# A convolutional-attention layer's preparation: all box differences on VectorE, and the first area addition behind the unit length of v

## The chip, the cores and the metric

The kernel runs on one core of one Trainium2 chip. A core has five engines with an instruction queue each: TensorE (PE in the profile; its weight loads are PEld), VectorE (DVE), ScalarE (ACT), GpSimd (POOL) and SyncE (SP, which here only starts transfers). An engine works through its queue in order and waits on semaphores for the others. The metric is the device time of one execution in microseconds (us). The time before is the median of three runs.

## The reference, cut to what matters

The input is an image of 256 channels and 64 x 64 places. A group normalisation goes ahead of layer 0, a box attention with 8 heads of 32 channels; layer 1 is a softmax attention over the 4096 places followed by a routed feed-forward layer with 8 experts. The change touches layer 0 alone:

```python
q = sigmoid(x . Wq);  k = sigmoid(x . Wk);  v = x . Wv / max(norm(v per head), 1e-12)
Ik  = integral(k)                   # sums over rows and columns
Ikv = integral(k[d] * v[f])         # the same for each product of channels
for w in (1, 2, 4):                 # box of 64/w x 64/w places, edges held
    wk, wkv = box(Ik), box(Ikv)     # four corners of the integral
    attn = sum_d q[d] * wkv[d, f]
    norm = sum_d q[d] * wk[d]
    outs.append(attn / (norm + 1e-6))
x = x + concat(outs) . Wout + bout
```

A box sum is taken by differences of prefix sums: along one axis, the prefix sum at the far end less the one at the near end; past the image's edge the last prefix sum (the "whole") stands for the far end.

## The kernel before

Layer 0 is done twice, for group 0 and group 1 of 128 channels (4 heads each): `prepare(g)` makes queries, keys, values and denominators, `attend(g)` the masked products within the boxes. The image is cut into NCH = 8 strips of SW = 8 columns; a strip is NB = 4 tiles of 16 x 8 = 128 places, each of two cells of 8 x 8. The three boxes reach REACH = 4, 2 and 1 strips to each side.

`prepare` consists of these steps, in the order of the program:

1. Keys and values (L441 on PE), eight times: the sigmoid of keys on ACT (L453), the copy of values on DVE (L454), their squares on POOL (L455), sums of squares on DVE (L456). After each half, a root on ACT (L459), then on DVE a maximum (L460), a reciprocal (L461) and the scaling of `v` to length 1 (L463, the whole half at once).
2. Sums of `k v` by cell (`sum_cells`, L418 on PE), in four parts. The last two parts need the second half of `v` scaled; they stand in PE's queue behind the area products 1 and 2. ACT copies them to `st` (L430).
3. Area products, one for each strip `ix` (L536 and L540 on PE): prefix sums of keys within the strip. DVE adds what lies left of the strip (`side`): L544 for the 64 rows, L547 for the row below, L549 for the next `side`. In group 0, strips 1 to 4 are followed by 8 transposes each (`residual`, L385), which are held behind that strip's L549 by `tc.issue_after(latest.ins)`. They read rows to which ACT has added a bias (L379).
4. Cell sums become prefix sums (`near`, L490 and L493 on DVE), then half boxes for reach 4 and 2: a copy on ACT (L503) and two differences (L506, L512) along each axis. In group 0 the two differences run on POOL, in group 1 on DVE:

```python
engine = nc.vector if g else nc.gpsimd
```

5. Query and key projections by channel (L476 on PE, a sigmoid on ACT, L483), four pairs of strips each.
6. For each reach, `tall` and `edge`: differences of the area along rows (an ACT copy L581, DVE L584 and L586). Then, for two blocks of four strips, `prod`: the difference along columns, times q. Where the near end lies left of the image there is no difference (L598, DVE). Elsewhere the difference is on POOL (L602 from the whole, L604 between two strips) and the product on DVE (L605). PE adds the products of all channels of a head into the denominators (L609), and DVE reads them when all three boxes are in (L622).

`prod` has two buffers, and shares them with `st` and the half boxes. `tall` has one. The PSUM tiles of steps 1, 2, 3 and 5 come from one ring of three (two banks each), so an area product needs the additions of an earlier one done.

Instructions are put on the engines' queues by a scheduler that goes by what is ready in its own estimate, so the order on DVE isn't the order of the program: in group 0, additions of strips 0 and 1 were put ahead of the second scaling of `v`. `tc.issue_after(x)` keeps what is recorded under it behind `x`. Transfers are not moved: SP's queue is the same before and after.

`attend` begins when the denominators are read (L622). Its masks are multiplied on DVE and POOL (L659), both before and after.

Of the kernel before, what the change touches and what calls it, by code (L numbers as in the profile page):

```python
# [30 lines left out]
P = 128  # L31
# [3 lines left out]
NT = N // P  # L35
CH = 512
NCH = N // CH
IMG = 64
SW = 8
# [3 lines left out]
D = 32  # L43
# [77 lines left out]
def tile_conv_attn_hybrid(ctx: ExitStack, tc: tile.TileContext, a: dict, out: bass.AP):  # L121
    nc = tc.nc
# [99 lines left out]
    def tok(i):  # L222
        return slice(P * i, P * (i + 1))
# [44 lines left out]
    with ExitStack() as phase:  # L268
# [124 lines left out]
        def prepare(g, w3, prep, ps):  # L393
# [41 lines left out]
            ss = prep.tile([P, 4 * NT], F32, name="ss")  # L435
            for i4 in range(0, NT, 4):
                pr = two_banks()
                kv = pr.rearrange("p j (i n o) -> p (j i) n o", i=2, n=2)
                for i in range(4):
                    for k in range(KC):  # L440
                        nc.tensor.matmul(  # L441
                            kv[:, i],
                            act[:, k, tok(i4 + i)],
                            w3[:, k, 1:3, :],
                            start=k == 0,
                            stop=k == KC - 1,
                        )
                at = slice(i4, i4 + 4)

                with ExitStack() as order:  # L450
                    if not g and i4 >= NT - 8:
                        order.enter_context(tc.issue_after(biased((i4 - NT + 8) // 4)))
                    nc.scalar.activation(kt[:, at, :], kv[:, :, 0, :], AF.Sigmoid)  # L453
                nc.vector.tensor_copy(v[:, at, :], kv[:, :, 1, :])  # L454
                nc.gpsimd.tensor_mul(sq[:, at, :], v[:, at, :], v[:, at, :])  # L455
                nc.vector.tensor_reduce(ss[:, 4 * i4 : 4 * (i4 + 4)], heads(sq[:, at, :]), AX.X, ALU.add)  # L456
                if i4 % 16 == 12:
                    half = slice(4 * (i4 - 12), 4 * (i4 + 4))
                    rooted = nc.scalar.sqrt(ss[:, half], ss[:, half])  # L459
                    nc.vector.tensor_scalar_max(ss[:, half], ss[:, half], 1e-12)  # L460
                    nc.vector.reciprocal(ss[:, half], ss[:, half])  # L461
                    to = heads(v[:, i4 - 12 : i4 + 4, :])
                    latest = nc.vector.tensor_mul(to, to, ss[:, half].unsqueeze(2).to_broadcast([P, 2 * NT, D]))  # L463
                if i4 >= NT - 8:
                    sum_cells((i4 - NT + 8) // 4)

# [19 lines left out]
            def near():  # L486


                for i in range(1, NCH):
                    nc.vector.tensor_add(st[:, i], st[:, i], st[:, i - 1])  # L490
                    yield
                for i in range(1, SW):
                    nc.vector.tensor_add(st[:, :, i], st[:, :, i], st[:, :, i - 1])  # L493
                    yield

                engine = nc.vector if g else nc.gpsimd

                def boxes(to, src, r, axis):

                    along = (lambda z, s: z[:, s]) if axis == 0 else (lambda z, s: z[:, :, s])  # L500
                    cut = lambda n: [P, n, SW, D] if axis == 0 else [P, SW, n, D]
                    last = lambda n: along(src, slice(SW - 1, SW)).to_broadcast(cut(n))
                    nc.scalar.copy(along(to, slice(0, r)), along(src, slice(r - 1, 2 * r - 1)))  # L503
                    n = SW + 1 - 2 * r
                    if n > 0:
                        engine.tensor_sub(  # L506
                            along(to, slice(r, r + n)),
                            along(src, slice(2 * r - 1, SW)),
                            along(src, slice(0, n)),
                        )  # L510
                    n = max(n, 0)
                    engine.tensor_sub(  # L512
                        along(to, slice(r + n, SW)), last(SW - r - n), along(src, slice(n, SW - r))
                    )

                for r in REACH[:2]:
                    half = prep.tile([P, NCH, SW, D], F32, tag="st", name="half", bufs=2)
                    boxes(half, st, r, 0)
                    yield
                    boxes(ssum[r], half, r, 1)  # L520
                    yield
# [6 lines left out]
            area = prep.tile([P, NCH, IMG + 1, SW], F32, tag="area", name="area")  # L528
            new_side = lambda: prep.tile([P, IMG + 1], F32, tag="side", name="side", bufs=2)
            side = new_side()  # L530
            nc.vector.memset(side, 0.0)
            for ix in range(NCH):
                pr = two_banks()
                for m in range(NB):
                    lhsT = kt[:, NB * ix + m, :]
                    nc.tensor.matmul(  # L536
                        pr[:, 0, P * m :], lhsT, ck["before8"][:, : CH - P * m], start=m == 0, stop=m == NB - 1
                    )
                    n = SW + IMG + 1
                    nc.tensor.matmul(  # L540
                        pr[:, 1, :n], lhsT, ck["sides"][:, n * m : n * (m + 1)], start=m == 0, stop=m == NB - 1
                    )
                left = side.unsqueeze(2).to_broadcast([P, IMG + 1, SW])
                nc.vector.tensor_add(  # L544
                    area[:, ix, :IMG, :], pr[:, 0, :].rearrange("p (y c) -> p y c", c=SW), left[:, :IMG]
                )
                nc.vector.tensor_add(area[:, ix, IMG, :], pr[:, 1, :SW], left[:, IMG])  # L547
                upto = new_side()
                add = nc.vector.tensor_add(upto, pr[:, 1, SW:n], side)  # L549
                side, latest = upto, add if ix else latest  # L550
                if ix in (1, 2):
                    sum_cells(ix + 1)
                if not g and 1 <= ix <= NB:
                    with tc.issue_after(latest.ins):
                        residual(ix - 1)
                for _ in range(3 if ix > 1 else 0):
                    next(steps, None)
# [11 lines left out]
            for w, r in enumerate(REACH):  # L569
# [18 lines left out]
                y_c = lambda z: z.rearrange("p (y c) -> p y c", c=SW)  # L588
                whole = edge.unsqueeze(2).to_broadcast([P, IMG, SW])
                for lo in range(0, NCH, 4):  # L590
                    prod = prep.tile([P, 4, CH], F32, tag="st", name="prod", bufs=2)
                    at = lo
                    while at < lo + 4:
                        first, last = at < r, at + r >= NCH
                        n = 1 if at + 1 in (r, NCH - r, lo + 4) else 2
                        to, of = prod[:, at - lo : at - lo + n], lambda by: sums[:, at + by : at + by + n]
                        if first:
                            nc.vector.tensor_mul(to, of(r), q[:, at : at + n])  # L598
                        else:
                            if last:  # L600
                                for j in range(n):
                                    nc.gpsimd.tensor_sub(y_c(to[:, j]), whole, y_c(of(-r)[:, j]))  # L602
                            else:
                                nc.gpsimd.tensor_sub(to, of(r), of(-r))  # L604
                            nc.vector.tensor_mul(to, to, q[:, at : at + n])  # L605
                        at += n
                    for i in range(lo, lo + 4):
                        n = NCH // 4 * w + i // 4
                        nc.tensor.matmul(  # L609
                            den[D * (i % 4) : D * (i % 4 + 1), :],  # L610
                            ck["sums"][:, D * n : D * (n + 1)],
                            prod[:, i - lo, :],
                            start=w == 0 and lo == 0,
                            stop=w == NW - 1 and lo > 0,
                            skip_group_check=True,
                        )
                    if later:
                        later.pop(0)()
# [18 lines left out]
        turns, latest, owed = [0], [None], [0]  # L637
# [234 lines left out]
        for g in range(KC):  # L872
            with tc.tile_pool(name="c_prep", bufs=1) as prep, psum("c_ps1", 2) as ps:
                of = prepare(g, w3, prep, ps)
# [284 lines left out]
    with ExitStack() as phase:  # L1159
# [590 lines left out]
        with tc.If(tame > 0) as branch:  # L1750
            with (
# [108 lines left out]
                held, latest, turned = [], [], []  # L1860
# [41 lines left out]
                r, i, room = slots.pop(0)  # L1902
                for cost, ops in pieces:
                    if cost is None:
                        while not (r % KC == KC - 1 and i in (13, 25)) or (r, i) in early:
                            r, i, room = slots.pop(0)
                        shared[r, i] = ops
                        r, i, room = slots.pop(0)
                        continue
                    if cost > room:  # L1910
                        r, i, room = slots.pop(0)
# [15 lines left out]
                for s, (r, i) in enumerate(places):  # L1927
                    qc, g = rounds[r]
# [34 lines left out]
                for n in range(CH // P):  # L1963
                    to = result(KC - 1, NCH - 1)[:, tok(n)]
# [5 lines left out]
        with branch.Else():  # L1970


            with (
# [8 lines left out]
                for hd in range(2 * 4):  # L1982
                    g, hs = hd // 4, slice(D * (hd % 4), D * (hd % 4 + 1))
# [116 lines left out]
```

## Time and profile before

| | |
|---|---|
| median of 3 runs | 2748.64 us (2747.01 to 2750.99) |
| the profiled execution | 2748.26 us, span 2746.5 us |
| mean granted TensorE clock | 0.984 |
| busy: PE, DVE, ACT, POOL | 96%, 68%, 55%, 32% of the span |
| POOL busy | 887.4 us in 953 instructions |
| preparation of group 0, from the first projection to the denominators (L441 to L622) | 22.3 to 143.4 us |
| preparation of group 1, the same | 517.5 to 623.5 us |
| layer 1 and what follows | from about 1042 us to the end |

A profile line names the line of the kernel, the engine, the operation and its tiles (out, then in) with partitions x elements. A mean of a group mixes shapes, so durations are best taken shape by shape. Starts and durations in the timeline are in us; what stands in brackets is the engine's idle time just before and what released it. Back to back, instructions of DVE overlap by some 0.1 us, so the sum of durations is a little more than the time they take. [...]

### The profile page before, as it was taken

The page shows a single profiled execution, that of the slowest core. Times are in us where ns is not written, and L with a number is a line of the kernel's source. Part 1 is how long each engine was busy: PE and PEld are TensorE (multiplying, and loading weights), DVE is VectorE, ACT ScalarE, POOL GpSimd, SP SyncE. Part 2 cuts the span into 40 slices and gives each one's busy share as a digit, 9 for nine tenths or more (in the row PEclk, how much of TensorE's full clock was granted, in tenths as well). Part 3 has the DMA queues.
Part 4 walks back from the last instruction along what each step waited for, and adds up shares of the span by engine and source line. Part 5 has one row for each costly group of instructions (what it writes and reads, how often), then busy time and mean ns, then how long its engine had stood idle before and what let it go on. Part 6 is the DMA issues. An engine that isn't in the chain of part 4 may idle for free.

```text
span 2746.5 us, 71816 instructions
## 1 busy us (share of the span) xinstructions
PE 2638.5 (96%) x30910; PEld 1187.3 (43%) x30910; DVE 1878.5 (68%) x2520; ACT 1503.2 (55%) x2083; POOL 887.4 (32%) x953
## 2 busy tenths in 40 slices
PE   6889999988999999999999999999999999999995
PEld 5454336745433655111212121212121278888884
DVE  5758788675868876788888889888888871111114
ACT  3223323222232334999898989898989852222222
POOL 2558777435777742000000100000001123222220
PEclk9899999999999999999999999999999999999996
DMA  5000000000000000455555555555656645555555
GB/s 146 7 23 21 15 26 24 8 13 23 24 12 28 22 21 1 99 118 117 112 113 113 116 113 113 113 113 116 132 113 132 159 142 180 190 187 178 187 175 194
DMA packets 114468, 256.66 MB, mean 93 GB/s; under 512 B 19890, under 2 KB 76440, under 8 KB 100052
## 3 DMA queue, kind: packets, MB, share of 16 engines
q0 software_dynamic: 22240, 132.66, 23.1%
q1 hardware_dynamic: 84724, 110.30, 12.4%
q10 hardware_dynamic: 7168, 8.92, 1.0%
q8 instruction: 247, 4.05, 0.6%
q14 instruction: 89, 0.73, 0.1%
HBM read 118.64 MB, written 17.86 MB: 50 GB/s over the span
## 4 chain that ended last, share of the span: by engine, by line
PE 90%; DVE 4%; DMA 3%; issue 1%; POOL 1%; ACT 0%; ACTq 0%; SPq 0%; DVEq 0%; POOLq 0%
PE ps_three L1805 19%; PE ps_acc L1764 18%; PE ps_sc L832 8%; PE ps_yp L1473 7%; PE ps_hp L1456 7%; PE ps_acc L848 7%; PE ps_sc L732 3%; PE ps_sc L759 3%; PE ps_acc L790 3%; PE ps_two L441 2%; PE ps_mm L1248 2%; DMA yrows<-v,qk 2%; PE ps_two L536 1%; PE ps_acc L778 1%; PE ps_two L476 1%
## 5 line engine op out<-in xcount | busy, mean ns | idle before, releaser
L1805 PE MATMUL ps_three<-qk 32*64 32x512 f32 x6144 | 564.0, 613 | 2.0 <-DVE t L1743 1.0
L1805 PE MATMUL ps_one<-qk 32*64 32x512 f32 x2048 | 557.2, 613 | 0.2 <-ACT pe L1814 0.2
L652 ACT COPY sm<-ps_sc 128x384 f32<-128x384 f32 (+3 forms) x454 | 218.5, 511 | 525.5 <-PE ps_sc L832 333.9
L1837 DVE TENSOR_TENSOR act<-act,pe 128x2048 f32<-128x2048 f32 x195 | 446.9, 2292 | 83.6 <-ACT pe L1817 53.1
L1817 ACT ACTIVATE pe<-ps_three 128x1536 f32<-128x1536 f32 x330 | 477.4, 1447 | 0.0
L1825 POOL DMA_DIRECT2D pe<-pe x108 | 93.3, 863 | 940.4 <-ACT pe L1817 654.6
L659 DVE TENSOR_TENSOR sm<-ps_sc,mask 128x512 f32<-128x512 f32 (+3 forms) x740 | 340.4, 520 | 68.4 <-PE ps_sc L832 65.2
L659 POOL TENSOR_TENSOR sm<-sm,mask 128x192 f32<-128x192 f32 (+3 forms) x428 | 350.1, 848 | 113.3 <-ACT sm L652 112.9
L1837 DVE TENSOR_TENSOR act<-act 128x2048 f32<-128x2048 f32 x150 | 343.9, 2292 | 51.1 <-ACT act L1817 37.9
L1764 PE MATMUL ps_acc<-pe,v 128*32 128x512 f32 x2640 | 352.4, 606 | 0.0
L1459 ACT ACTIVATE v<-ps_hp,qk 128x256 f32<-128x256 f32 (+1 forms) x256 | 123.0, 480 | 343.5 <-PE ps_hp L1456 340.7
L1805 PEld LDWEIGHTS ps_three<-qk 32*64 32x64 f32 x6144 | 112.8, 130 | 415.0 <-ACT pe L1814 242.3
L1817 ACT ACTIVATE act<-ps_three 128x1536 f32<-128x1536 f32 x182 | 263.1, 1446 | 0.0
L1473 PE MATMUL ps_yp<-qk,v 128*128 128x256 f32 (+1 forms) x1088 | 241.7, 380 | 0.0
L1456 PE MATMUL ps_hp<-qk 128*128 128x256 f32 (+1 forms) x1024 | 237.6, 389 | 2.8 <-ACT v L1459 1.7
L832 PE MATMUL ps_sc<-qk 32*64 32x384 f32 (+3 forms) x3584 | 235.2, 458 | 0.5 <-issue 0.5
L1814 ACT ACTIVATE pe<-ps_one 128x512 f32<-128x512 f32 x330 | 197.4, 598 | 60.9 <-PE ps_one L1805 36.8
L1473 PEld LDWEIGHTS ps_yp<-qk,v 128*128 128x128 f32 (+1 forms) x1088 | 200.3, 187 | 30.7 <-issue 1.3
L848 PE MATMUL ps_acc<-sm,v 128*32 128x256 f32 (+3 forms) x2688 | 213.2, 419 | 0.2
L1456 PEld LDWEIGHTS ps_hp<-qk 128*128 128x128 f32 x1024 | 181.0, 189 | 53.3 <-ACT v L1459 14.2
L1764 PE MATMUL ps_acc<-act,v 128*32 128x512 f32 x1456 | 193.9, 604 | 0.0
L659 DVE TENSOR_TENSOR sm<-ps_sc,ycut 128x384 f32<-128x384 f32 (+4 forms) x254 | 129.1, 560 | 81.5 <-PE ps_sc L759 79.8
(365 smaller groups left out, 2946.3 us busy)
## 6 DMA issues: line engine op xcount, KB each, us to landing
pe<-pe POOLq DMA_DIRECT2D x108, 1024.0 KB
qk<-in_L_ffn_W SPq DMA_DIRECT2D x64, 1024.0 KB
by<-recs SPq DMA_DIRECT2D x48, 256.0 KB
rows<-in_x SPq DMA_DIRECT2D x16, 256.0 KB
qk<-in_L_ffn_b SPq DMA_DIRECT2D x32, 128.0 KB
y<-yrows SPq DMA_DIRECT2D x8, 512.0 KB
y<-yrows ACTq DMA_DIRECT2D x8, 512.0 KB
rec<-recs SPq DMA_DIRECT2D x60, 64.0 KB
```

The lines of the kernel that those rows point to most:

```text
L652: copied = nc.scalar.copy(sm[:, :used], sc[:, :used])
L659: done = engine.tensor_mul(to, of, mk.unsqueeze(1).to_broadcast(list(to.shape)))
L832: nc.tensor.matmul(scs[h][u : u + rows, at : at + n], kT[hs[h], P * i + u : P * i + u + rows], qT[hs[h], CH * ix + CELL * c0 : CH * ix + C ...
L848: nc.tensor.matmul(acc[hs[h], CELL * c0 : CELL * c1], v[:, i, hs[h]], sms[h][:, at : at + n], start=not begun[0], stop=last and at == plac ...
L1456: nc.tensor.matmul(hp[:, :n], w1[:, k, tok(m)], x_now[:, k, :n], start=k == 0, stop=k == KC - 1)
L1459: done["gelu"] = nc.scalar.activation(hid[:, m, :n], hp[:, :n], AF.Gelu, bias=cols[:, m : m + 1]).ins
L1473: product = nc.tensor.matmul(yp[:n], hid[:, m, P * j : P * j + n], w2[:, m, :], start=m == 0, stop=m == NH - 1)
L1764: nc.tensor.matmul(to[D * hd : D * (hd + 1), :], lhsT(hd), rhs(hd), start=start, stop=stop, skip_group_check=True,)
L1805: nc.tensor.matmul(to[CELL * u : CELL * (u + 1), :], qk[hs, 1, g, P * i + CELL * u : P * i + CELL * (u + 1)], qk[hs, 0, g, chunk(qc)], sta ...
L1814: first = nc.scalar.activation(head(pe, 0), one, AF.Exp, scale=C**-0.5)
L1817: nc.scalar.activation(pe[:, CH:], three.rearrange("p h n -> p (h n)"), AF.Exp, scale=C**-0.5).ins
L1837: latest[:] = [nc.vector.tensor_add(total, total, weights_of[r, i]).ins]
```

## The change

All differences of the preparation go to DVE: L506 and L512 in group 0 as they are in group 1 already, and L602 and L604 in both groups. The products with q stay where they are, one for each difference. The first addition of area (strip 0, L544) is held behind the scaling of the second half of `v`, which now has the name `unit_v`. `latest` is always the last L549; only strips from 1 on use it, for which it was that before.

```diff
-                    latest = nc.vector.tensor_mul(to, to, ss[:, half].unsqueeze(2).to_broadcast([P, 2 * NT, D]))
+                    unit_v = nc.vector.tensor_mul(to, to, ss[:, half].unsqueeze(2).to_broadcast([P, 2 * NT, D]))
...
-                engine = nc.vector if g else nc.gpsimd
...
-                        engine.tensor_sub(
+                        nc.vector.tensor_sub(
                             along(to, slice(r, r + n)),
                             along(src, slice(2 * r - 1, SW)),
                             along(src, slice(0, n)),
                         )
                     n = max(n, 0)
-                    engine.tensor_sub(
+                    nc.vector.tensor_sub(
                         along(to, slice(r + n, SW)), last(SW - r - n), along(src, slice(n, SW - r))
                     )
...
-                nc.vector.tensor_add(
-                    area[:, ix, :IMG, :], pr[:, 0, :].rearrange("p (y c) -> p y c", c=SW), left[:, :IMG]
-                )
+                with nullcontext() if ix else tc.issue_after(unit_v.ins):
+                    nc.vector.tensor_add(
+                        area[:, ix, :IMG, :], pr[:, 0, :].rearrange("p (y c) -> p y c", c=SW), left[:, :IMG]
+                    )
...
-                side, latest = upto, add if ix else latest
+                side, latest = upto, add
...
-                                    nc.gpsimd.tensor_sub(y_c(to[:, j]), whole, y_c(of(-r)[:, j]))
+                                    nc.vector.tensor_sub(y_c(to[:, j]), whole, y_c(of(-r)[:, j]))
                             else:
-                                nc.gpsimd.tensor_sub(to, of(r), of(-r))
+                                nc.vector.tensor_sub(to, of(r), of(-r))
                             nc.vector.tensor_mul(to, to, q[:, at : at + n])
```

The scheduler places the rest anew. On DVE in group 0, the second scaling of `v` now stands ahead of all area additions, and each of the first area additions is followed by one or two cell additions; the first three blocks of transposes keep their places behind strips 1, 2 and 3, and the fourth stands within strip 6 instead of within strip 5. The half boxes come within and behind strip 7, mixed with the first `tall`. On PE two of the denominators' products of the second box move ahead of the last projection.

## The prediction

> **What bounds the kernel now.** I read the page's engine shares and chain first: TensorE (PE) carries 90% of the chain, VectorE 4%, GpSimd (POOL) 1%. That average says little about the two preparations, so I took the busy time by stretch. Columns: stretch (us), its length, busy us of PE, weight load, DVE (VectorE), ACT, POOL with counts, granted PE clock, DMA share, GB/s.
>
> ```profile
> 56.00:88.80 32.80, 28.91 (x382) 21.36 (x381) 25.48 (x74) 9.01 (x22) 0.00 (x0) 0.90 0.01 2
> 88.80:143.40 54.60, 43.64 (x110) 13.82 (x108) 41.22 (x25) 15.62 (x19) 42.08 (x21) 0.84 0.03 8
> ...
> 579.00:623.50 44.50, 37.51 (x106) 12.08 (x104) 31.14 (x25) 12.70 (x15) 24.92 (x13) 0.88 0.06 18
> ```
>
> The second and third rows are the ends of the two preparations (group 0, group 1). PE is busy 80 to 84% of them, its clock is reduced, and POOL works as long as DVE. Which of them ends last is read from the chain in order of time (start, us, what), here for group 0:
>
> ```profile
> 60.59 0.69 DVE area L544
> 61.45 0.51 DVE ss L461
> 62.04 2.25 DVE v L463
> 64.43 1.53 PE ps_two L418 x85
> 65.97 2.00 PE ps_two L536 x2
> ...
> 88.85 2.51 POOL half L506
> ...
> 105.45 5.17 POOL prod L602 x4
> 110.64 2.29 DVE tall L584
> ...
> 130.09 2.87 POOL prod L604
> 132.97 7.24 DVE prod L605 x3
> 140.25 3.14 PE ps_mm L609 x8
> 143.42 0.70 DVE rec L622
> ```
>
> Two things. At 60 to 64 PE waits for `v`, because two area additions stand ahead of the second scaling of `v`; the next area products then run slowly. From 88.85 to 143.42 the chain passes between POOL and DVE and is on PE only at the end. Third, what these two cost each other, in DVE's and POOL's order of time in group 1:
>
> ```profile
> 604.63 1.23 DVE L605 TENSOR_TENSOR prod<-prod,qk 128x1024 f32<-128x1024 f32 x1 [0.97 <-POOL prod L602]
> 612.79 9.30 DVE L605 TENSOR_TENSOR prod<-prod,qk 128x1024 f32<-128x1024 f32 x5 [2.23 <-POOL prod L604]
> 609.90 9.03 POOL L604 TENSOR_TENSOR prod<-tall 128x1024 f32<-128x1024 f32 x4 [5.30 <-ACT root L880]
> ```
>
> With POOL idle a 1024-wide product takes 1.23 us. The five products at 612.79 (two of 1024, three of 512 wide) would take 2 x 1.23 + 3 x 0.69 = 4.5 us; beside POOL they take 9.30.
>
> [...] products of 1024 take 2.08 beside POOL and 1.22 without. [...] Here an undisturbed 1024-wide POOL subtraction took 2.34 (at 599.21) against 1.22 on DVE; a 512-wide one took 1.07 against 0.69. [...] after the 3.9 us wait for `v` the clock of 64 to 70 us is 0.53, and the first pair of 512-wide area products takes 2.07 instead of 1.07 to 1.13.
>
> **Part 1, group 0: `v` before the area additions.** In the changed program DVE's order is scale of `v`, then area 0, side 0, a cell sum, area 1. The root on ACT ends at 56.57; 0.2 (maximum) + 0.55 (reciprocal) + 2.29 follow, so `v` is ready near 59.7 instead of 64.3. PE finishes area product 1 at 60.55 as before and goes straight on: cell sums 1.25 us, an area product 3.05 us (the spacing from 72.2 on). Area product 2 ends at 64.9, was 71.0. Five products and the last cell sums follow: PE ends them at 81.4, was 87.65. Part 1 alone is worth 6.2 us to PE. The cost is area 0 at 59.7 instead of 57.5; its PSUM pair isn't needed again until 61.9, and it is read by 60.5. ACT's second copies of cell sums come at 66.3 and the last 8 biased rows by 70.7, so transposes are not held.
>
> **Part 2, the half-box differences of group 0.** Eight operations leave POOL, which spends 16.5 us on them (88.85 to 105.4, all on the chain). On DVE the same shapes are seen in group 1, 568.8 to 578.7: 0.43 + 0.95 + 0.42 + 0.95 + 1.48 + 0.42 + 1.48 + 0.42 = 6.55.
>
> **Part 3, the product differences, both groups.** Each group has 7 of 512, 4 of 1024 and 2 of 512 wide (13 operations; 25.9 us on POOL in group 0, 24.9 in group 1). On DVE: 9 x 0.69 + 4 x 1.22 = 11.1 us. Back to back, starts are some 0.09 closer than durations (area 544 starts at 75.73, 547 at 76.33), so 0.60 and 1.14 apiece: 10.0. Those on DVE that POOL stretched go back to their own length. The DVE work of 88.8 to 143.4, priced at undisturbed rates (large subtractions 7.5, edges 1.0, first products 4.4, L605 7 x 1.22 + 3 x 0.69 = 10.6, the denominators' read 0.7, the first large one 2.3), is 26.5 of the 41.2 busy: 14.7 us were contention.
>
> **Sum, group 0.** From 59.7 DVE has: 8 area triples x 0.81 = 6.5, 14 cell additions x 0.43 = 6.0, 32 transposes 10.6 (2.64 per 8), half boxes 6.3, large differences and edges 10.0, first products 4.0, multiplications 7 x 1.14 + 3 x 0.6 = 9.8, differences 10.0. That is 63.2, so 122.9 if nothing waits. Waits I find by walking the new order against PE and ACT: 0.7 for area products 2, 3 and 5, and 0.9 at the second half box, which reuses a buffer that ACT's copy reads until about 89.2. Query sigmoids are ready at 88.2, 90.2, 93 and 96.3 and the products need them at 93, 94, 97 and 99; not held. Last multiplication ends near 124.4, was 142.3. The masked stage begins at the denominators' read (L622), 1.1 us after: 125.5 instead of 143.4. **Gain 17.9.** PE's share ends by 113.9, so DVE sets this end. Cover gone: every later DVE microsecond here costs one.
>
> **Sum, group 1.** Up to 581.4 nothing of weight changes: half boxes were on DVE, area products weren't held, and `v` is scaled by 553.5 with PE at 554.3. Then PE's projections lead (query pairs end at 579.5, 583.0, 586.4, 589.9), and hide the differences of the first box in gaps where DVE waited for POOL. The second box begins at 594.45 when PE has read the product buffer, as now. Its second difference waits for the other buffer until 599.0; the box ends at 603.8. The large subtraction takes 3.27 + 0.61, and the third box 8.8: end near 616.5, was 622.1. With the same 1.3 to L622, 617.8 instead of 623.46. **Gain 5.7.** PE waits longer between the last denominators, as it does now, so this stays on DVE.
>
> Together 23.6. No queue is passed by a moved DMA: SP's order is unchanged. What follows (masked attention, layer 1) starts from these two ends, so it moves as a block. Profiled run 2748.26 with span 2746.5: it would be 2724.7. The median shown, 2748.64, is 0.4 above it: 2725.
>
> **Rivals.** (a) *Half of it*: DVE carries all, and the waits I set at 1.6 us are several times longer (ACT copies feed the half boxes in group 0, buffers of products are held by denominators). For it: ACT's copies wait 2.9 us at a time for their input today. Against: each such copy is 0.6 to 1.0 us and I found room at each. If group 0 yields 9 and group 1 3 us: 2737. (b) *Nothing*: POOL's differences are cover that DVE now lacks. In group 1 alone there is a case, since PE is on the chain until 607 whatever DVE does. But the last stretch, 609.9 to 622, is POOL and DVE in series, and group 0 has 16.5 us of POOL alone on the chain. To give 2748, group 0 must gain nothing. (c) *Slower*: at group 0's area products DVE falls so far behind that a PSUM pair isn't read when PE needs it again. For it: from 61 to 82 us DVE has 10.6 us of transposes in blocks of 2.64 and 5.5 us of cell additions, where PE hands it an area product every 3.05 us. The price of one such stall is what the wait for `v` costs now: 3.9 us of waiting and some 2.0 of slow products behind it, 5.9. At each of products 3 to 7 it makes 29.5, L622 at 155 instead of 143.4; less group 1's 5.7 that is 2754.5. It decides from the fourth stall on: four (23.6) cancel the whole gain. Against: there are three pairs, so DVE must lag by some 5 us before PE feels it, and my walk has at most 1, at area 7. (d) *The change moves nothing*: excluded: in the changed program's order POOL has no difference left.
>
> **Numbers.** Full gain 0.70, with its own range 2720 to 2731: undisturbed prices are sure to 0.05 us each, over 26 operations 1.3 us per group; dependent pairs start 0.12 later, up to 2 us; on the other side, a wait of PE that I let stand. (a) 0.19, (b) 0.03, (c) 0.05, the rest 0.03 for other slow cases. Range 2719 to 2738: it holds the full gain and most of (a). Faster by over 0.2% (5.5 us, what can be told from no change here) 0.90, within 0.03, slower 0.07.
>
> **What would show it.** POOL has no work between 56 and 127 us. L605 of 1024 is 1.22 everywhere. L418 at about 60.6 without a wait; the clock of 60 to 110 stays at 1.0. L622 at about 125.5; in group 1, from its first projection (517.5 now) to L622, 100.3 us instead of 105.9. Wrong would be: area additions after PE by more than 3 us; half boxes waiting on ACT; differences of 512 and 1024 on DVE longer than 0.7 and 1.25; a stage after the preparations that takes longer than now and eats the gain.

## The result, and the profile after

The changed kernel takes 2726.32 us (median of 4 runs, 2723.66 to 2727.95) against 2749.81 for the kernel before beside it (2747.01 to 2751.12). The ratio is 0.9915, 95% interval 0.9898 to 0.9932: 23.5 us faster, where 23.6 was forecast. Measured a second time, it took 2724.11 against 2747.24, ratio 0.9916 (0.9903 to 0.993).

The profiled execution has a span of 2726.2 us. First the busy time of the three stretches shown of before, with borders at the same points of the program: the area products, the boxes of group 0, the boxes of group 1 (stretch, length, busy us of PE, weight load, DVE, ACT, POOL, granted PE clock as a share of full speed, DMA share, GB/s).

```profile
57.32:84.70 27.38, 27.38 (x384) 20.53 (x383) 25.45 (x74) 8.95 (x22) 0.00 (x0) 1.00 0.01 2
84.70:127.76 43.06, 38.49 (x108) 12.51 (x107) 40.21 (x48) 15.87 (x19) 0.00 (x0) 0.92 0.04 10
563.55:602.58 39.03, 34.66 (x106) 11.86 (x104) 34.27 (x38) 12.56 (x15) 0.00 (x0) 1.00 0.07 21
```

PE is busy through the whole first stretch at full clock. In the second, DVE is busy 40.2 of 43.1 us and POOL does nothing. DVE's busy time there is almost what it was before (41.2), though it does 48 instructions instead of 25: the work taken over is about as large as the blocking that went (DVE operations that took longer beside POOL's, such as the product of 1024 at 107.59 of before: 2.08 us, where it takes 1.21 now, at 98.32).

The chain in order of time, for group 0 (start, us, what):

```profile
61.86 1.22 PE ps_two L418 x80
63.08 1.06 PE ps_two L534 x2
...
83.65 0.69 DVE area L543
...
90.57 1.49 DVE half L504
...
96.59 1.26 DVE prod L601 x3
...
106.16 2.27 DVE prod L603 x2
108.43 2.27 DVE prod L604 x2
...
124.26 3.48 PE ps_mm L608 x8
127.76 0.70 DVE rec L621
```

The cell sums (L418) follow area product 1 with no wait for `v`, and the next pair of 512-wide products takes 1.06 instead of 2.00 in the chain. POOL is gone from it. The denominators are read at 127.76 instead of 143.42.

And the same five last products of a group, with three of their differences, in DVE's order of time (group 1). A row of x2 is one operation of 1024 and one of 512:

```profile
594.82 1.82 DVE L604 TENSOR_TENSOR prod<-prod,qk 128x1024 f32<-128x1024 f32 x2
596.56 1.82 DVE L603 TENSOR_TENSOR prod<-tall 128x1024 f32<-128x1024 f32 x2
598.29 1.81 DVE L604 TENSOR_TENSOR prod<-prod,qk 128x1024 f32<-128x1024 f32 x2
600.03 0.68 DVE L601 TENSOR_TENSOR prod<-edge,tall 128x512 f32<-128x512 f32 x1
600.75 0.69 DVE L604 TENSOR_TENSOR prod<-prod,qk 128x512 f32<-128x512 f32 x1
```

The products alone took 9.30 us here beside POOL; now they take 1.82 + 1.81 + 0.69 = 4.3, and with their five differences they run from 593.08 to 601.44, 8.4 us. So products and differences together need less than the products did.

To see where the time went, the execution is cut at three places that exist in every kernel here: the first projection of a group (L441), its first cell sums (L418), and the denominators' read (L621, before L622).

| us | before | after | after, measured again |
|---|---|---|---|
| start to first projection, group 0 | 22.3 | 22.1 | 22.8 |
| first projection to first cell sums, group 0 | 25.8 | 27.4 | 25.8 |
| first cell sums to denominators, group 0 | 95.3 | 78.3 | 77.8 |
| masked products of group 0 | 374.1 | 374.7 | 374.0 |
| preparation of group 1 | 105.9 | 100.1 | 99.7 |
| the rest (span less all above) | 2123.1 | 2123.6 | 2122.2 |

The change is worth 17.0 us in group 0 and 5.9 in group 1 (17.5 and 6.3 with the second profile), and nothing is lost behind it. The second row is untouched by the change and swings between 25.7 and 27.4 us over the twelve profiles made here. The first profile after fell on a long one, and its masked products and its rest came out some 0.6 us longer each, so its span is only 20.3 us shorter than that of before while the medians are 23.5 apart. Group 0 is therefore counted from the first cell sums below.

### The profile page after: what moved, and what is told of

It reads as the page before. It is cut to its first block, busy times and chain, and to the rows that moved or that the text cites. A ratio compares the mean times of both kernels' runs of the same rounds, so it can differ in the third digit from the quotient of the medians.

```text
span 2726.2 us, 71805 instructions
## 1 busy us (share of the span) xinstructions
PE 2626.7 (96%) x30910; PEld 1184.6 (43%) x30910; DVE 1879.7 (69%) x2554; ACT 1502.6 (55%) x2083; POOL 820.7 (30%) x919
## 3 DMA queue, kind: packets, MB, share of 16 engines
q1 hardware_dynamic: 84724, 110.30, 12.5%
## 4 chain that ended last, share of the span: by engine, by line
PE 90%; DVE 4%; DMA 3%; issue 1%; ACT 0%; POOL 0%; ACTq 0%; SPq 0%; DVEq 0%; POOLq 0%
PE ps_three L1804 19%; PE ps_acc L1763 19%; PE ps_sc L831 8%; PE ps_yp L1472 8%; PE ps_hp L1455 7%; PE ps_acc L847 7%; PE ps_sc L731 3%; PE ps_sc L758 3%; PE ps_acc L789 3%; PE ps_two L441 2%; PE ps_mm L1247 2%; DMA yrows<-v,qk 2%; PE ps_two L534 1%; PE ps_acc L777 1%; PE ps_three L1738 1%
## 5 line engine op out<-in xcount | busy, mean ns | idle before, releaser
L658 POOL TENSOR_TENSOR sm<-sm,ycut 128x384 f32<-128x384 f32 (+4 forms) x146 | 147.1, 1028 | 225.4 <-ACT sm L651 224.9
```

Of the source, the lines that this page charges most:

```text
L658: done = engine.tensor_mul(to, of, mk.unsqueeze(1).to_broadcast(list(to.shape)))
```

## The experiments

The theory, in three parts: (1) the second scaling of `v`, late on DVE, held PE; (2) POOL's half boxes were on the chain; (3) POOL's differences and DVE's products blocked each other. The rivals: POOL's work was cover and its removal only shifts the bound; what cost time was waiting for POOL's slow results and not blocking; DVE's load in the area stretch stalls PE.

### One part of the change at a time

The kernel before with the hold of the first area addition alone:

```diff
-                nc.vector.tensor_add(
+                with nullcontext() if ix else tc.issue_after(unit_v.ins):
+                    nc.vector.tensor_add(
```

> The kernel before, with the first area addition behind the scaling of v, and nothing else. Theory (the parts add up, and the area products were held by v): PE's wait for v goes, the clock between the area products stays at 1.0, the last area product ends about 6 us earlier counted from the first projection; DVE's prefix sums of cells, which start POOL's half boxes, come some 5 us earlier, so group 0's preparation (first projection to the denominators' read, 121.1 us before) takes 115 to 117 and the kernel is about 5 us faster. Rival (the wait for v is slack, since POOL and DVE set the end of group 0): the area products end earlier and the denominators are read at the same time as before, within 1 us. Group 1 stays at 106.0 in both.

Measured: 2743.42 against 2748.77 us, ratio 0.9981 (0.9973 to 0.9988). From the first cell sums to the denominators 90.5 us instead of 95.3, so 4.8 us; group 1 took 105.3. PE went on to the query projections 33.30 us after the first cell sums, was 39.35, and each of its pairs of 512-wide area products took 1.07 to 1.13 us, none the 2.07 of before; POOL began the half boxes 5.4 us earlier. The rival falls: the wait for `v` was on the path, although POOL and DVE stood behind it. From the first projection the stretch was 116.3, in the expected 115 to 117.

The half boxes of group 0 alone:

```diff
-                engine = nc.vector if g else nc.gpsimd
+                engine = nc.vector
```

> The kernel before, with group 0's half boxes on DVE, and nothing else. Theory: 16.5 us of POOL on the chain become 6.5 of DVE. DVE wants to be at the first product about 98.5 instead of 99.7, is no longer stretched there, and POOL starts the first box's differences at about 98 instead of 105.5; the contention of the boxes is unchanged behind it. Group 0's preparation 121.1 to about 114, the kernel 7 us faster. Rival (DVE is the bound there, so what POOL gives up DVE only takes over): less than 2 us. Group 1 stays at 106.0.

Measured: 2745.72 against 2748.77, ratio 0.9988 (0.9979 to 0.9997). Group 0 took 91.4 instead of 95.3: 3.9 us, not 7. Neither expectation is met. Its DVE and POOL in order of time show why:

```profile
99.99 3.23 DVE L598 TENSOR_TENSOR prod<-tall,qk 128x1024 f32<-128x1024 f32 x2
104.19 2.08 DVE L605 TENSOR_TENSOR prod<-prod,qk 128x1024 f32<-128x1024 f32 x1 [0.97 <-POOL prod L602]
```

```profile
100.22 6.99 POOL L602 TENSOR_TENSOR prod<-edge,tall 128x512 f32<-128x512 f32 x4 [43.44 <-DVE ssum L512]
```

POOL starts the first box's differences 5.2 us earlier (100.22, was 105.45; 6.5 us counted from the first cell sums), but now beside DVE's first two products. The four take 6.99 instead of 5.16, and the two products 3.23, still more than the 2.35 that they take alone. Part of the gain goes back into blocking as long as the differences stay on POOL.

The differences along columns alone, in both groups:

```diff
-                                    nc.gpsimd.tensor_sub(y_c(to[:, j]), whole, y_c(of(-r)[:, j]))
+                                    nc.vector.tensor_sub(y_c(to[:, j]), whole, y_c(of(-r)[:, j]))
                             else:
-                                nc.gpsimd.tensor_sub(to, of(r), of(-r))
+                                nc.vector.tensor_sub(to, of(r), of(-r))
```

> The kernel before, with the differences along columns on DVE in both groups, half boxes of group 0 still on POOL, v as before. Theory: group 1 takes all of its gain from this: 106.0 becomes 100.1, as in the changed kernel. Group 0: the half boxes still end near 105.4, then DVE needs the 29.6 us that the changed kernel takes from the first difference to the last product, so the last product ends at about 135 instead of 142.3: 7 us. Together 13 faster; the products of 1024 take 1.22 us wherever POOL is idle. Rival (POOL's work was cover): group 1 is not faster, or loses, since PE leads it until the last projection.

Measured: 2735.26 against 2748.77, ratio 0.9946 (0.993 to 0.9963), 13.5 us. Group 1 took 100.8 instead of 105.9 (5.2 of the whole 5.9), group 0 89.2 instead of 95.3 (6.1). The rival that POOL's work was cover falls in both groups.

And the changed kernel without the hold:

```diff
-                with nullcontext() if ix else tc.issue_after(unit_v.ins):
-                    nc.vector.tensor_add(
+                nc.vector.tensor_add(
```

> The changed kernel with the first area addition free again, so that two area additions stand ahead of the scaling of v as before the change; all differences stay on DVE. Theory (PE's wait for v delays the area products by 6 us, and DVE, which has more to do than before, finds them late): group 0 counted from its first cell sums takes 4 to 5 us longer than the changed kernel's 78.3, as much as the hold was worth alone (4.8). Rival (with all differences on DVE, DVE can work ahead, and the wait for v is hidden): under 1.5 us longer. Group 1 stays at 100.

Measured: 2730.29, ratio 0.9935 (0.992 to 0.995); group 0 83.2, group 1 100.5. The hold is worth 4.9 us at this end (5.4 against the second profile), 4.8 alone: within 0.6 us it is independent of the rest. Its wait is back as it was, 3.89 us, with a pair of 2.07 us behind it where others take 1.07 (PE's order of time):

```profile
66.12 1.54 PE L418 MATMUL ps_two<-v,kt 64*32 64x32 f32 x128 [3.89 <-DVE v L463]
67.59 2.07 PE L534 MATMUL ps_two<-cstk,kt 128*128 128x512 f32 x2
```

Half boxes and differences together are then 95.3 - 83.2 = 12.1 us in group 0, where they gave 3.9 + 6.1 = 10.0 apart.

### Blocking, or waiting for results

The changed kernel, with work on POOL that no engine waits for. Once it reads:

```diff
+            spare = prep.tile([P, CH], F32, name="spare")
+            mark = prep.tile([P, NW], F32, name="mark")
+            nc.gpsimd.memset(spare, 1.0)
...
+                nc.vector.tensor_copy(mark[:, w : w + 1], edge[:, :1])
+                nc.gpsimd.tensor_copy(spare[:, :1], mark[:, w : w + 1])
+                for _ in range((4, 6, 7)[w]):
+                    nc.gpsimd.tensor_sub(spare, spare, spare)
```

> The changed kernel, and beside the boxes of each group POOL does 17 subtractions of 512 elements on a spare tile that no other engine touches (4, 6 and 7 for the three boxes; one small copy on DVE and one on POOL start each). No engine waits for POOL's result. Theory (a DVE operation with two SBUF inputs is blocked by POOL operations that read SBUF): DVE's products and differences are stretched as before the change, by about one POOL operation each: 8 to 18 us longer in group 0 and 5 to 15 in group 1. Rival (what cost time was only waiting for POOL's results, which take longer to make): under 1 us.

and once it only writes:

```diff
-                    nc.gpsimd.tensor_sub(spare, spare, spare)
+                    nc.gpsimd.memset(spare, 1.0)
```

> As the kernel with POOL's spare subtractions, but POOL writes a constant to the spare tile 17 times per group and reads nothing apart from the three small starting copies. Theory (only reads contend): group times within 1 us of the changed kernel, the products of 1024 at 1.22. Rival (any work of POOL slows DVE): several microseconds longer.

Measured with reads: 2751.34 us, ratio to the kernel before 1.0006 (0.9997 to 1.0015). Group 0 took 91.8 (13.5 more than the changed kernel), group 1 111.6 (11.5 more): the spare subtractions alone give the whole gain back. With writes: 2726.22, ratio 0.9915 (0.9896 to 0.9935); 77.8 and 99.7, as the changed kernel. The products of 1024 in group 0, by form (count, busy us, mean ns, idle before), with reads and then with writes:

```profile
L611 DVE TENSOR_TENSOR prod<-prod,qk 128x1024 f32<-128x1024 f32 x7 | 11.0, 1575 | 0.0
```

```profile
L611 DVE TENSOR_TENSOR prod<-prod,qk 128x1024 f32<-128x1024 f32 x7 | 8.5, 1221 | 0.0
```

DVE has next to no idle time before them in either, so it doesn't wait for POOL: the instructions themselves get longer. The third box of the kernel with reads shows both cases in one execution:

```profile
120.67 13.79 POOL L595 TENSOR_TENSOR spare<-spare 128x512 f32<-128x512 f32 x7
126.63 3.50 DVE L610 TENSOR_TENSOR prod<-tall 128x1024 f32<-128x1024 f32 x2
136.06 1.82 DVE L611 TENSOR_TENSOR prod<-prod,qk 128x1024 f32<-128x1024 f32 x2
```

While POOL reads, a pair of 1024 and 512 takes 3.50 us; after POOL's last subtraction, at 134.46, such a pair takes 1.82. POOL gets slower too: its seven subtractions take 1.97 us each there on average, where a difference of 512 alone took 1.07 before the change (L602). In the kernel that only writes, POOL was busy for 12.5 us in the boxes of group 0 against 35.7, so the two differ in load as well; but DVE's operations beside the writes, such as two products of 1024 in 2.35 us at 92.92, kept their length. Blocking is enough by itself to make the loss, and POOL's reads do it where its writes don't.

This doesn't show that waiting cost nothing. The same products before the change, in group 0 and then in group 1:

```profile
L605 DVE TENSOR_TENSOR prod<-prod,qk 128x1024 f32<-128x1024 f32 x7 | 13.1, 1893 | 5.0 <-POOL prod L602 2.8 <-POOL prod L604 2.2
L605 DVE TENSOR_TENSOR prod<-prod,qk 128x1024 f32<-128x1024 f32 x7 | 11.4, 1645 | 7.9 <-POOL prod L604 6.9 <-POOL prod L602 1.0
```

They were both stretched and kept waiting. Summed over the 24 DVE instructions of the boxes that exist in both kernels, durations fell from 42.6 to 25.7 us in group 0 and from 32.5 to 25.7 in group 1, and the waits for POOL ahead of them were 12.1 and 10.9 us and are gone. So in group 0 blocking was the larger part (16.9 us) and in group 1 waiting was (10.9 against 6.8). The rival is wrong that blocking cost nothing; that waiting cost something is right.

### Is DVE the bound

The changed kernel with the transposes done twice:

```diff
                         residual(ix - 1)
+                        residual(ix - 1)
```

> The changed kernel with each of group 0's 32 transposes done twice (the second writes the same values again): 10.6 us more for DVE in the stretch of the area products. Theory (DVE alone is the bound of group 0): the denominators' read comes 10 to 11 us later. PE will feel the lag near the last area products, by two waits of about 3 us, but it has 10 us of room behind. Rival (the stall that would have made the change slower): the waits lower PE's clock, its projections stretch, and the end moves by 15 us or more.

Measured: 2732.17, ratio 0.9938 (0.9919 to 0.9958). Group 0 took 87.3, which is 9.0 us more than the changed kernel's 78.3 (9.5 more than its second profile), a little under the expected 10 to 11. The times differ by less, 0.9938 against 0.9915 or some 6 us, with intervals of 0.2% on either side. The stall is there, in PE's order of time:

```profile
83.41 2.04 PE L534 MATMUL ps_two<-cstk,kt 128*128 128x512 f32 x2 [3.33 <-DVE side L548]
...
90.44 17.40 PE L476 MATMUL ps_two<-act,w 128*128 128x512 f32 x40 [2.32 <-issue]
```

PE waits 3.33 us for a PSUM pair at the last area product, and the first pair of matmuls behind it takes 2.04 us instead of 1.07. Before the query projections it stands idle for another 2.32. Neither costs anything beyond DVE's own lag: the end moved by less than the 10.6 us of added work. So the mechanism of the slower rival exists, after 8 us of added work, but there is room behind it.

The changed kernel with the first 8 transposes taken out of that stretch:

```diff
+                if not g and i4 == NT - 4:
+                    residual(0)
...
-                if not g and 1 <= ix <= NB:
+                if not g and 2 <= ix <= NB:
```

> The changed kernel, with group 0's first 8 transposes taken out of the area additions and put into DVE's gaps beside the last projections of keys and values. Theory (DVE alone sets the end of group 0 from the area additions on, so every microsecond off it counts): 2.6 us off group 0's preparation, 105.7 in the changed kernel. The scaling of v must not come later than PE needs it, for which there is 0.9 us. Rival (the end is set by PE, ACT or by buffers as much as by DVE): under 1 us.

Measured: 2723.38, ratio 0.9903 (0.9887 to 0.992). Group 0 took 76.8: 1.5 us less than the changed kernel's first profile and 1.0 less than its second, between the two expectations. DVE's order of time shows where the rest stayed:

```profile
61.49 0.87 DVE L492 TENSOR_TENSOR st<-st 128x256 f32<-128x256 f32 x2
64.93 0.69 DVE L545 TENSOR_TENSOR area<-ps_two,side 128x512 f32<-128x512 f32 x1 [2.57 <-PE ps_two L540]
```

The time taken out opened as a wait for area product 2. So PE and DVE are nearly equal limits up to strip 7. That DVE alone is one behind it is borne out by the kernel with POOL's reads: from the last area addition on, DVE was busy for 55.3 us instead of 41.2, and the denominators came 13.5 us later. Moving the second and third 8 transposes up as well fills that gap:

```diff
-                if not g and 2 <= ix <= NB:
+                if not g and 1 <= ix < NB:
                     with tc.issue_after(latest.ins):
-                        residual(ix - 1)
+                        residual(ix)
```

> The changed kernel with all of group 0's transposes a strip earlier: the first 8 beside the last key projections, the second and third 8 behind strips 1 and 2, the last 8 still within strip 6. With only the first 8 moved, DVE waited 2.6 us for area product 2, and the half boxes began with less gain than the 2.6 us taken out. Theory (up to strip 7 PE and DVE are nearly equal limits, and DVE's work only counts where it fills a gap): the gap at strip 2 is filled, the cell sums and the first half box go ahead of area 7, and group 0 counted from its first cell sums takes 75 to 76 us, against 76.8 with the first 8 moved and 78.3 in the changed kernel. Rival (PE sets that stretch and what follows): no change against 76.8.

Measured: 2720.65 against the changed kernel's 2724.11 beside it; ratios to before 0.9904 (0.9889 to 0.9919) and 0.9916. Group 0 took 75.3, in the expected range, and 2.5 less than the changed kernel's 77.8. The wait at strip 2 is 0.42:

```profile
65.76 0.69 DVE L545 TENSOR_TENSOR area<-ps_two,side 128x512 f32<-128x512 f32 x1 [0.42 <-PE ps_two L540]
```

This is the fastest version tried, by 3.5 us in the medians. The intervals of the ratios overlap, but the four times (2718.98 to 2722.29) all lie below the changed kernel's five (2722.53 to 2726.60).

The changed kernel itself, beside those two:

> The changed kernel as it is, beside the other two on the same chip. Expected: 0.990 to 0.993 of the kernel before, group 0 counted from its first cell sums 77.5 to 78.5 us, group 1 100 us. The first projections, which the change doesn't touch, may take 25.7 to 27.4 us up to those cell sums, as they do in the profiles so far.

Measured: 2724.11, ratio 0.9916; 77.8 and 99.7, with 25.8 to the first cell sums. All as expected.

## Why the prediction was right

Point by point, by its own steps:

- **Part 1.** Forecast: 6.2 us earlier for PE. Counted from the first cell sums, PE was through the area products after 33.30 us, was 39.35: 6.05. Group 0's gain from this part was 4.8 to 5.4. The chain behind starts from DVE, which came forward less than PE: with the hold alone, the half boxes began 5.4 us earlier. The wait and the slow pair behind it are gone, as said, and the clock from 60 to 110 us is 1.00.
- **Part 2.** The prices were met: the eight half-box differences on DVE took 0.42 + 0.95 + 0.42 + 0.95 + 1.49 + 0.42 + 1.49 + 0.42 = 6.56 us. The wait of 0.9 for ACT's copy was there, 0.94.
- **Part 3.** The prices were met: 1.22 and 0.68. All seven 1024-wide products of group 0 average 1219 ns, were 1893. The 14.7 us put down to contention in group 0 were too low: the same instructions lost 16.9 us of duration. This estimate was no term of the sum, which was built from undisturbed prices.
- **Sum, group 0.** Forecast 17.9, measured 17.0 from the first cell sums; 17.5 in the second profile. On the forecast's own scale, from the start of the span, the denominators' read came at 127.76 instead of 125.5, since the first projections took some 1.3 us longer. The last term is another part of the difference: between the last product and the denominators' read there were 1.63 us instead of 1.1 in the first profile (the product ended at 126.13), with PE's clock at 0.81 from 110 us on: six matmuls of denominators behind a wait of 1.82 us took 2.52. In the second profile six behind a wait of 1.83 us took 1.65, and the wait for the read was 1.14. What lowered the clock in the first was not shown.
- **Sum, group 1.** Forecast 5.7 (100.3 us left), measured 100.1 and 99.7. The waits for the product buffers, 1.92 and 1.01 us, were where the walk had them: counted from the group's first projection, the second box began after 76.5 us and its second difference after 81.1 (76.9 and 81.5 in the walk).
- **That the gain passes through as a block.** The stretches behind changed by some 0.6 us each.
- **The total.** That it was met within 0.1 us is luck: the two preparations gained 22.9 us in the first profile and 23.8 in the second, and the medians 23.5 and 23.1. What the forecast had right is each group's gain, to within 1 us.
- **Where a step was wrong.** "Every later DVE microsecond here costs one" held only behind strip 7. Up to there, 2.6 us less were worth 1.0 to 1.5 and 10.6 more cost 9.0 to 9.5. The total didn't suffer because the walk had PE and DVE side by side anyway. And "POOL works as long as DVE" was read from group 0 (42.1 and 41.2 us); in group 1 POOL worked 24.9 us to DVE's 31.1.
- **Rivals.** "Half of it" needed waits several times as long as the 1.6 us in the walk. "Nothing" is refuted by the differences on DVE alone, 13.5 us faster. "Slower" needed four stalls; with the transposes doubled PE waited twice, and both were hidden. My threshold of 5 us was about right: there, PE didn't feel that DVE read area product 3 4.0 us late, but it felt 7.7 us at product 4. Its price was not: I priced a stall at PE as if it reached the end, and PE has room there.

What stays open: why half boxes and differences give 2.1 us more together than apart. The first box's differences beside the first products, seen in one profile, are a likely reason, but it was not isolated further. How the gain divides between blocking and waiting was summed from the traces, not measured by a run of its own. What decides the length of the first projections was not tried.

## What to carry to other kernels

An operation isn't free on GpSimd merely because GpSimd is idle. Here GpSimd operations that read SBUF beside VectorE operations with two SBUF inputs made both longer (1.22 to 2.06 us for a product of 1024, 1.07 to 1.97 for a GpSimd subtraction of 512), and VectorE ended sooner doing the work of both (8.4 us for five products and their differences, where the products alone took 9.30). Look for it in a trace by comparing the duration of one form with the other engine busy and idle, before counting anything as hidden. And when a stretch is called bound by an engine, walk the second engine too: work taken off the first is worth only what the second leaves (here 1.0 to 1.5 of 2.6 us).

## What the runs showed of the hardware that I had not expected

- The blocking was no shorter for a small operation, and it went both ways. Before the change, a VectorE subtraction of 8 elements took 2.34 us beside GpSimd's large subtractions; after the change the same takes 0.16:

```profile
114.24 5.47 POOL L604 TENSOR_TENSOR prod<-tall 128x1024 f32<-128x1024 f32 x2 [3.63 <-DVE tall L586]
117.40 2.34 DVE L586 TENSOR_TENSOR edge<-side 128x8 f32<-128x8 f32 x1
```

  It ended at 119.74, just behind GpSimd's second subtraction (119.71). In the kernel whose POOL only writes, one operation of POOL still reads, a copy of one element per partition. In group 0 it took 1.04 to 1.40 us, and each time it ended some 0.04 us behind the two-input operation of VectorE beside it; in group 1, with no such operation running when it started, it took 0.18:

```profile
91.18 1.48 DVE L504 TENSOR_TENSOR ssum<-half 128x1280 f32<-128x1280 f32 x1
91.31 1.40 POOL L593 COPY spare<-mark 128x1 f32<-128x1 f32 x1 [35.74 <-DVE mark L592]
...
575.53 0.18 POOL L593 COPY spare<-mark 128x1 f32<-128x1 f32 x1 [5.14 <-DVE mark L592]
```

- The first 112 records of projections took 25.9 us before and 27.4 after, with the same instructions in the same order. From 22 to 28 us PE worked on 22 of them in the one and on 17 in the other; from 30 to 48 us it was 85 in both, and the granted clock was 1.00 throughout. From 24 to 26 us it was 7 and 6, from 26 to 28 us 11 and 6, from 28 to 30 us 11 and 10. That the slow start lasts some 1.5 us longer in some executions is a difference larger than several of the effects measured here, and it would have hidden the size of parts 1 and 2 in a comparison of spans.
